# A selective-scan layer on one core: channels in four groups of 32 partitions, row and column tiles of the array, the C product on GpSimd, B left in PSUM

## The chip, the core and the metric

The kernel runs on one core of a Trainium2 chip. The metric is the device time of one execution in microseconds (us), lower being better. Five engines matter: PE (TensorE: matmuls, with its weight loads listed apart as PEld), DVE (VectorE), ACT (ScalarE), POOL (GpSimd) and SP (SyncE, which issues most of the DMAs). Each works through its own instructions in order, and they wait for one another by semaphores. PE writes its results to PSUM; the other tiles of the kernel lie in SBUF.

## What is computed

The reference is a small network on 4 images of 64 x 64 positions and 96 channels: two state-space layers ("SS2D"), then two layers of attention without softmax and a quantised feed-forward. Only the two state-space layers are touched by the change. One of them is, for every image:

```python
xz = einsum('bhwc,ec->bhwe', groupnorm(x), in_proj_w)       # 96 -> 2 x 192 channels
xx, z = split(xz, 2);  z = silu(z)
xc = silu(depthwise_conv3x3(xx) + conv_b)                   # 192 channels
for k in range(4):                # rows, columns, both backwards: u = xc in that order
    dts, Bm, Cm = split(x_proj_weight[k] @ u, [6, 22])      # 6 + 16 + 16
    delta = softplus(dt_projs_weight[k] @ dts + dt_bias[k]) # 192 channels
    h = exp(delta * A) * h + delta * Bm * u                 # 192 channels x 16 states, step by step
    y += sum_over_states(h * Cm) + Ds[k] * u
x = x + out_proj(layernorm(y) * z)
```

All of it is in float32. The recurrence for h runs over the 4096 positions of an image, in 4 directions, for 192 channels with 16 states each.

## The kernel before

**Staging.** `ssm_layer` runs twice, each time over 4 images. Per image there is `conv` (groupnorm, then the input projection and the depthwise convolution as one 3x3 convolution of nine matmuls per output, giving `xc`), then 32 steps (4 directions k x 8 chunks c of TC = 512 positions), then `finish` (layernorm, gate, output projection, residual). The attention and feed-forward layers follow in `token_layers`.

**Layout.** The 192 inner channels are two halves h of C = 96, on 96 partitions. A scan tile has 128 partitions: EG = 8 channels x 16 states, for 512 positions. A half has NJ = 12 scan tiles, so a chunk has 24, and the kernel has 2 x 4 x 32 x 24 = 6144.

**`chunk_inputs`** prepares one chunk. Four matmuls give B and C, each row repeated for the 8 channels of a scan tile (L216); ACT copies both to the SBUF tile `bc` (L220). Four more give the raw step (L225), and softplus is made of it by ACT (L239 to L243), DVE (L244) and two POOL instructions (L245, L247): `delta`. DVE multiplies `delta` by u (L250), and one DMA writes that to DRAM (`scratch`, L252). The views of u have steps of one element in directions 0 and 2, and of a whole row in directions 1 and 3.

**`scan_chunk`** does the 24 scan tiles. Every four tiles one DMA brings `dur`, delta * u spread over the states (L264). Per tile j:

- L272, PE: `da` = `rep[:, j]` x `delta`: a matmul of 96 rows that copies the 8 channels of tile j to their 128 partitions;
- L273, ACT: `da` = exp(`da` x A), in place in PSUM;
- L275, DVE: `st` = `dur` x B;
- L277, DVE: the scan itself, `st` = `da` h + `st`; L281, ACT, keeps the last column as `carry` for the next chunk;
- L282, DVE: `st` = `st` x C;
- L283, PE: `y_ps` += `sel` x `st`: sums the 16 states and puts the 8 channels in their places among the 96 (twelve matmuls accumulate).

At the end of a half DVE adds `y_ps` to `y` (L297; L293 in direction 0).

**Order.** The source calls `chunk_inputs` of the next chunk before `scan_chunk` of this one. The order on each engine is fixed when the program is built, by the framework's scheduler, which lists instructions by the order of the source and by when their operands and buffers would be ready. Waits and buffer counts decide the rest: `da` has 3 PSUM buffers, `y_ps` 2, the pair of B and C (and the pair of raw steps) one buffer of two PSUM banks, the pool `p_one` 1; `st` has 4 SBUF buffers, `dur` 3, `delta` and `bc` 2. That is all 8 PSUM banks.

**In the trace** every float32 matmul appears as two passes with a weight load each, so 6144 matmuls are listed as x12288.

Of the kernel before, what the change touches and what calls it, by code (L numbers as in the profile page):

```python
# [18 lines left out]
B = 4            # images  # L19
HW = 64          # rows and columns of an image  # L20
L = HW * HW      # positions of an image
C = 96           # model channels
E = 192          # inner channels of the scan, as two halves of C
NS = 16          # states per inner channel
R = 6            # rank of the step projection
K = 4            # scan directions
PAD = HW + 2
TC = 512         # positions per chunk
NC = L // TC
ROWS = TC // HW  # L30
EG = 8           # inner channels of one scan tile: 8 channels x 16 states
NJ = C // EG     # scan tiles per half
JG = 4           # scan tiles whose inputs one load brings
HID = 384        # FFN
# [6 lines left out]
def scan_view(t, k, c):  # L41
    """Chunk c of the scan order of direction k, of a tile [C, 2, L] in image order:
    [C, 2, ROWS, HW]. 0: rows; 1: columns; 2, 3: the same backwards."""
    part, half = t.ap[0], t.ap[1]
    if k == 0:
        off, steps = TC * c, (HW, 1)
    elif k == 1:
        off, steps = ROWS * c, (1, HW)
    elif k == 2:
        off, steps = L - 1 - TC * c, (-HW, -1)  # L50
    else:
        off, steps = L - 1 - ROWS * c, (-1, -HW)
    return bass.AP(t.tensor, t.offset + off, [part, half, [steps[0], ROWS], [steps[1], HW]])


def rows(t):
    """The last dim, of TC positions, as ROWS x HW."""
    if len(t.shape) == 2:
        return t.rearrange("p (r w) -> p r w", w=HW)
    return t.rearrange("p h (r w) -> p h r w", w=HW)  # L60


class Consts:
    def __init__(self, nc, pool, a):
# [4 lines left out]

        self.rep = load("rep", [C, NJ, 128])  # L70
        self.sel = load("sel", [128, C + NJ - 1])
        self.group = load("group", [C, C])
        self.mask = load("mask", [C, C])
        self.mean_e = pool.tile([C, C], F32, name="mean_e")
        nc.vector.memset(self.mean_e, 1.0 / E)
# [8 lines left out]
def neg_rsqrt(nc, cst, var, ln, r, sq):  # L84
    """r = -(var + EPS) ** -0.5: an exponential's first guess and one Newton step."""
    nc.scalar.activation(ln, var, AF.Ln, bias=cst.eps[:C])
# [7 lines left out]
def ssm_layer(ctx: ExitStack, tc, cst, a, pre, x_in, x_out):  # L94
    """x_out = x_in + SS2D(groupnorm(x_in)), images as [C, L]."""
# [8 lines left out]
    p_y = ctx.enter_context(tc.tile_pool(name=pre + "p_y", bufs=2, space=PSUM))  # L104
    p_two = ctx.enter_context(tc.tile_pool(name=pre + "p_two", bufs=1, space=PSUM))
    p_one = ctx.enter_context(tc.tile_pool(name=pre + "p_one", bufs=1, space=PSUM))

# [1 line left out]
    in_w = wp.tile([C, 2 * E], F32, name="in_w")  # L109
    nc.sync.dma_start(in_w, a[pre + "in_proj_w"])  # L110
    taps = wp.tile([C, 9, E], F32, name="taps")
    nc.sync.dma_start(taps, a[pre + "conv_w"].unsqueeze(0).broadcast_to([C, 9, E]))
    conv_b = wp.tile([C, 2], F32, name="conv_b")
    nc.sync.dma_start(conv_b, a[pre + "conv_b"])
    dt_b = wp.tile([C, K, 2], F32, name="dt_b")
    nc.sync.dma_start(dt_b, a[pre + "dt_projs_bias"])
    ds_k = wp.tile([C, 2, K], F32, name="ds_k")
    nc.sync.dma_start(ds_k, a[pre + "Ds"])
    gam = wp.tile([C, 2], F32, name="gam")
    nc.sync.dma_start(gam, a[pre + "gamma"])  # L120
    bet = wp.tile([C, 2], F32, name="bet")
    nc.sync.dma_start(bet, a[pre + "beta"])
    out_w = wp.tile([C, 2, C], F32, name="out_w")
    nc.sync.dma_start(out_w, a[pre + "out_proj_w"])
    a_col = wp.tile([128, K, 2, NJ], F32, name="a_col")
    nc.sync.dma_start(a_col, a[pre + "A_logs"])
    xp_t = wp.tile([C, K, 2, R + 2 * NS], F32, name="xp_t")
    nc.sync.dma_start(xp_t, a[pre + "x_proj_t"])
    xp_dt = wp.tile([R, K, E], F32, name="xp_dt")
    nc.sync.dma_start(xp_dt, a[pre + "x_proj_dt"])  # L130
    dt_w = wp.tile([R, K, E], F32, name="dt_w")
    nc.sync.dma_start(dt_w, a[pre + "dt_projs_weight"])

    # The input projection and the depthwise convolution are one 3x3 convolution.
    nc.vector.tensor_tensor(
        taps, taps, in_w[:, :E].unsqueeze(1).broadcast_to([C, 9, E]), ALU.mult
    )
    # A = -exp(A_logs), a column for each scan tile.
    nc.scalar.activation(a_col, a_col, AF.Exp)
    nc.vector.tensor_scalar_mul(a_col, a_col, -1.0)  # L140
    ds = wp.tile([C, 2], F32, name="ds")
    nc.vector.tensor_reduce(ds, ds_k, AX.X, ALU.add)
    # B and C come out of the projection once for each of a scan tile's channels.
    bc_w = wp.tile([C, K, 2, 2, 128], F32, name="bc_w")
    dl_w = wp.tile([C, K, 2, E], F32, name="dl_w")
    for k in range(K):
        for h in range(2):
            nc.vector.tensor_copy(
                bc_w[:, k, h].rearrange("p m (n e) -> p (m n) e", e=EG),
                xp_t[:, k, h, R:].unsqueeze(2).broadcast_to([C, 2 * NS, EG]),  # L150
# [3 lines left out]
                ps[:C, :E], xp_dt[:, k, h * C : (h + 1) * C], dt_w[:, k, :], start=True, stop=True  # L154
            )
            nc.scalar.copy(dl_w[:, k, h], ps[:C, :E])
# [3 lines left out]
    def conv(b):  # L160
        """Groupnorm, projection, convolution and silu: xc, [C, 2, L]."""
# [12 lines left out]
        # Means over a group's channels: of the means, then of the squares around that.  # L174
# [16 lines left out]
        xc = big.tile([C, 2, L], F32, name="xc")  # L191
        for c in range(NC):
            for h in range(2):
                ps = p_one.tile([128, TC], F32, name="ps1")
                for tap in range(9):
                    dy, dx = divmod(tap, 3)
                    nc.tensor.matmul(  # L197
                        rows(ps[:C]),
                        taps[:, tap, h * C : (h + 1) * C],
# [5 lines left out]
                    xc[:, h, c * TC : (c + 1) * TC], ps[:C], AF.Silu, bias=conv_b[:, h : h + 1]  # L205
# [3 lines left out]
    def chunk_inputs(xc, k, c):  # L209
        """Of one chunk of a direction, in scan order: the steps delta, B and C, and in  # L210
        DRAM delta * u."""
        u = scan_view(xc, k, c)
        bc_ps = p_two.tile([128, 2, TC], F32, name="ps2")
        for m in range(2):
            for h in range(2):
                nc.tensor.matmul(  # L216
                    rows(bc_ps[:, m]), bc_w[:, k, h, m], u[:, h], start=h == 0, stop=h == 1
                )
        bc = cp.tile([128, 2, TC], F32, name="bc", bufs=2)
        nc.scalar.copy(bc, bc_ps)  # L220

        raw = p_two.tile([128, 2, TC], F32, name="ps2")
        for m in range(2):
            for h in range(2):
                nc.tensor.matmul(  # L225
                    rows(raw[:C, m]),
                    dl_w[:, k, h, m * C : (m + 1) * C],
                    u[:, h],
                    start=h == 0,
                    stop=h == 1,  # L230
                )
        # softplus(s) = max(s, 0) + log1p(e), e = exp(-|s|); with w = 1 + e as it rounds,
        # log1p(e) = ln(w) + (e - (w - 1)).
        top = cp.tile([C, 2, TC], F32, name="t0")
        e = cp.tile([C, 2, TC], F32, name="t1")
        ln = cp.tile([C, 2, TC], F32, name="t2")
        w = cp.tile([C, 2, TC], F32, name="t3")
        for m in range(2):
            nc.scalar.activation(top[:, m], raw[:C, m], AF.Relu, bias=dt_b[:, k, m : m + 1])  # L239
            nc.scalar.activation(e[:, m], raw[:C, m], AF.Abs, bias=dt_b[:, k, m : m + 1])  # L240
        nc.scalar.activation(e, e, AF.Exp, scale=-1.0)
        nc.scalar.activation(ln, e, AF.Ln, bias=cst.one[:C])  # L242
        nc.scalar.activation(w, e, AF.Identity, bias=cst.one[:C])  # L243
        nc.vector.scalar_tensor_tensor(w, w, -1.0, e, ALU.add, ALU.subtract)  # L244
        nc.gpsimd.tensor_tensor(ln, ln, w, ALU.subtract)  # L245
        delta = cp.tile([C, 2, TC], F32, name="delta", bufs=2)
        nc.gpsimd.tensor_tensor(delta, top, ln, ALU.add)  # L247
        du = cp.tile([C, 2, TC], F32, name="du")
        for h in range(2):
            nc.vector.tensor_tensor(rows(du[:, h]), rows(delta[:, h]), u[:, h], ALU.mult)  # L250
        scratch = dp.tile([2, C, TC], F32, name="scratch")
        nc.sync.dma_start(scratch.rearrange("h q t -> q h t"), du)  # L252
        return bc, delta, scratch

    def scan_chunk(k, c, bc, delta, scratch, carry, xc, y):
        """h = exp(delta A) h + delta u B along the chunk, partitions being 16 states x 8
        channels; y += C h, summed over the states on the tensor engine."""
        src = scratch.rearrange("h (e j) t -> h e j t", j=NJ)
        for h in range(2):
            y_ps = p_y.tile([128, TC], F32, name="y_ps")  # L260
            for j in range(NJ):
                if j % JG == 0:
                    dur = cp.tile([128, JG, TC], F32, name="dur", bufs=3)
                    nc.sync.dma_start(  # L264
                        dur.rearrange("p j t -> p (j t)"),
                        src[h, :, j : j + JG, :]
                        .rearrange("e j t -> e (j t)")
                        .unsqueeze(0)
                        .broadcast_to([NS, EG, JG * TC]),
                    )  # L270
                da = p_da.tile([128, TC], F32, name="da")
                nc.tensor.matmul(da, cst.rep[:, j], delta[:, h], start=True, stop=True)  # L272
# [300 lines left out]
```

## Time and profile before

| | |
|---|---|
| time, median of 3 runs | 21090.39 us (21075.26 to 21090.78) |
| span of the profiled execution, first to last instruction | 21085.4 us |
| busy: PE, DVE, ACT, POOL | 18224.8, 17258.1, 8714.3, 1244.7 us |
| mean granted clock of TensorE | 0.914 |
| DMA, mean over the span | 85 GB/s |

No time of the profiled execution apart from its span is listed; the span lies 5 us under the median of the runs. The profile's pages give the busy time of each engine, groups of instructions by line with their mean duration, the idle time ahead of them and what ended it, and a chain of waits: followed back from the last instruction, at each step to what released it. A matmul's end is modelled, not measured, so a busy PE need not be PE at its peak: the distance from one pass's start to the next one's is the safer reading.

### The profile page before, as it was taken

The page shows a single profiled execution, that of the slowest core. Times are in us where ns is not written, and L with a number is a line of the kernel's source. Part 1 is how long each engine was busy: PE and PEld are TensorE (multiplying, and loading weights), DVE is VectorE, ACT ScalarE, POOL GpSimd, SP SyncE. Part 2 cuts the span into 40 slices and gives each one's busy share as a digit, 9 for nine tenths or more (in the row PEclk, how much of TensorE's full clock was granted, in tenths as well). Part 3 has the DMA queues.
Part 4 walks back from the last instruction along what each step waited for, and adds up shares of the span by engine and source line. Part 5 has one row for each costly group of instructions (what it writes and reads, how often), then busy time and mean ns, then how long its engine had stood idle before and what let it go on. Part 6 is the DMA issues. An engine that isn't in the chain of part 4 may idle for free.

```text
span 21085.4 us, 115668 instructions
## 1 busy us (share of the span) xinstructions
PE 18224.8 (86%) x34144; PEld 5598.9 (27%) x34144; DVE 17258.1 (82%) x21566; ACT 8714.3 (41%) x15985; POOL 1244.7 (6%) x556
## 2 busy tenths in 40 slices
PE   8989889998989889897899889898898988998554
PEld 2222222222222222222222222222222222222222
DVE  6999599995999679995999869995899959997333
ACT  3444344443444344443444434443444434444555
POOL 0000000000000000000000000000000000000000
PEclk9999899998999899998999999998999989998666
DMA  3444244442444234442444334442444424443000
GB/s 85 99 102 98 57 102 100 101 94 62 100 101 100 64 92 98 102 97 60 100 100 100 87 71 100 101 98 59 100 99 102 98 54 101 100 101 74 14 6 6
DMA packets 352144, 1785.52 MB, mean 85 GB/s; under 512 B 85022, under 2 KB 86240, under 8 KB 154136
## 3 DMA queue, kind: packets, MB, share of 16 engines
q1 hardware_dynamic: 344344, 1765.54, 36.6%
q10 hardware_dynamic: 7168, 12.59, 0.2%
q8 instruction: 271, 4.44, 0.1%
q14 instruction: 361, 2.96, 0.1%
HBM read 1658.45 MB, written 119.54 MB: 84 GB/s over the span
## 4 chain that ended last, share of the span: by engine, by line
DVE 57%; PE 19%; ACT 14%; issue 9%; POOL 1%; DMA 0%; SPq 0%; ACTq 0%; DVEq 0%; POOLq 0%
DVE st L277 26%; DVE st L282 13%; DVE st L275 13%; PE ps L225 5%; PE ps L197 5%; PE da L272 2%; PE y_ps L283 2%; DVE du L250 1%; ACT L242 1%; ACT L273 1%; ACT t L239 1%; ACT L87 1%; ACT t L242 1%; ACT t L243 1%; ACT t L240 1%
## 5 line engine op out<-in xcount | busy, mean ns | idle before, releaser
L272 PE MATMUL da<-delta,rep 96*128 96x512 f32 x12288 | 6845.6, 646 | 779.6 <-DVE st L277 535.4
L283 PE MATMUL y_ps<-st,sel 128*96 128x512 f32 x12288 | 6623.4, 641 | 792.1 <-DVE st L282 661.9
L277 DVE TENSOR_TENSOR_SCAN st<-da,carry,st 128x512 f32<-128x512 f32 x5376 | 6745.7, 1270 | 143.8 <-ACT da L273 142.9
L273 ACT ACTIVATE da<-da,a_col 128x512 f32<-128x512 f32 x6144 | 4012.0, 660 | 4513.1 <-PE da L272 4500.9
L275 DVE TENSOR_TENSOR st<-dur,bc 128x512 f32<-128x512 f32 x6144 | 4035.2, 672 | 527.6 <-PE y_ps L283 445.4
L282 DVE TENSOR_TENSOR st<-st,bc 128x512 f32<-128x512 f32 x6144 | 4419.2, 733 | 30.1 <-ACT carry L281 27.6
L272 PEld LDWEIGHTS da<-delta,rep 96*128 96x128 f32 x12288 | 2058.4, 194 | 5583.1 <-DVE st L277 4298.6
L283 PEld LDWEIGHTS y_ps<-st,sel 128*96 128x96 f32 x12288 | 1815.2, 170 | 5393.4 <-DVE st L282 4274.6
L281 ACT COPY carry<-st 128x1 f32<-128x1 f32 x5376 | 1021.8, 191 | 4961.8 <-DVE st L277 4954.2
L245 POOL TENSOR_TENSOR t<-t,t 96x1024 f32<-96x1024 f32 x256 | 613.1, 2395 | 17479.5 <-DVE t L244 17418.4
L216 PE MATMUL ps<-xc,bc_w 96*128 96x512 f32 x2048 | 1417.2, 812 | 0.0
L225 PE MATMUL ps<-xc,dl_w 96*96 96x512 f32 x2048 | 1368.2, 813 | 0.0
L244 DVE SCALAR_TENSOR_TENSOR t<-t,t 96x1024 f32<-96x1024 f32 x256 | 312.5, 1221 | 1156.2 <-ACT t L243 1155.3
L197 PE MATMUL ps<-xn,taps 96*96 96x512 f32 x2304 | 1040.2, 606 | 31.0 <-DVE xn L190 24.8
L277 DVE TENSOR_TENSOR_SCAN st<-da,st 128x512 f32<-128x512 f32 x768 | 903.1, 1205 | 18.6 <-ACT da L273 18.6
L247 POOL TENSOR_TENSOR delta<-t,t 96x1024 f32<-96x1024 f32 x256 | 599.3, 2341 | 20.1
L216 PEld LDWEIGHTS ps<-xc,bc_w 96*128 96x128 f32 x2048 | 398.9, 195 | 690.3 <-issue 688.1
L225 PEld LDWEIGHTS ps<-xc,dl_w 96*96 96x96 f32 x2048 | 351.4, 173 | 860.5 <-issue 779.3
L197 PEld LDWEIGHTS ps<-xn,taps 96*96 96x96 f32 x2304 | 370.6, 165 | 683.4 <-issue 565.6
L250 DVE TENSOR_TENSOR du<-delta,xc 96x512 f32<-96x512 f32 x512 | 417.1, 853 | 158.0 <-POOL delta L247 158.0
L239 ACT ACTIVATE t<-ps,dt_b 96x512 f32<-96x512 f32 x512 | 347.5, 679 | 389.6 <-PE ps L225 389.1
L89 DVE SCALAR_TENSOR_TENSOR t<-ps,t 96x512 f32<-96x512 f32 x64 | 44.0, 687 | 534.2 <-ACT t L88 534.2
(117 smaller groups left out, 7565.8 us busy)
## 6 DMA issues: line engine op xcount, KB each, us to landing
dur<-scratch SPq DMA_DIRECT2D x1536, 1024.0 KB, 7.1
scratch<-du SPq DMA_DIRECT2D x256, 384.0 KB, 3.0
xr<-in_x SPq DMA_DIRECT2D x64, 192.0 KB, 2.5
x<-xr ACTq DMA_DIRECT2D x64, 192.0 KB, 2.1
xr<-x SPq DMA_DIRECT2D x64, 192.0 KB, 2.5
xn<-in_x SPq DMA_DIRECT2D x32, 192.0 KB, 3.9
xn<-x SPq DMA_DIRECT2D x32, 192.0 KB, 5.1
t<-x SPq DMA_DIRECT2D x4, 1536.0 KB, 8.9
```

The lines of the kernel that those rows point to most:

```text
L197: nc.tensor.matmul(rows(ps[:C]), taps[:, tap, h * C : (h + 1) * C], xn[:, ROWS * c + dy : ROWS * (c + 1) + dy, dx : dx + HW], start=tap == ...
L216: nc.tensor.matmul(rows(bc_ps[:, m]), bc_w[:, k, h, m], u[:, h], start=h == 0, stop=h == 1)
L225: nc.tensor.matmul(rows(raw[:C, m]), dl_w[:, k, h, m * C : (m + 1) * C], u[:, h], start=h == 0, stop=h == 1,)
L245: nc.gpsimd.tensor_tensor(ln, ln, w, ALU.subtract)
L250: nc.vector.tensor_tensor(rows(du[:, h]), rows(delta[:, h]), u[:, h], ALU.mult)
L272: nc.tensor.matmul(da, cst.rep[:, j], delta[:, h], start=True, stop=True)
L273: nc.scalar.activation(da, da, AF.Exp, scale=a_col[:, k, h, j : j + 1])
L275: nc.vector.tensor_tensor(st, dur[:, j % JG], bc[:, 0], ALU.mult)
L277: nc.vector.tensor_tensor_scan(st, da, st, 0.0 if c == 0 else col, ALU.mult, ALU.add)
L281: nc.scalar.copy(col, st[:, TC - 1 : TC])
L282: nc.vector.tensor_tensor(st, st, bc[:, 1], ALU.mult)
L283: nc.tensor.matmul(y_ps[:C], cst.sel[:, NJ - 1 - j : NJ - 1 - j + C], st, start=j == 0, stop=j == NJ - 1,)
```

## The change

The 192 channels are laid out anew: two halves of P = 128 partitions, each of NT = 4 groups of 32 partitions of which 24 carry channels (NB = 3 blocks of 8) and 8 are zero padding. Weights are padded on the host accordingly. Tile j = i * NT + t is block i of group t. Then:

- the matmul that makes `da` reads only the 32 partitions of group t (32 rows x 128 columns: a row tile of the array at row 32 t);
- the matmul that sums the states writes only the 32 partitions of group t (128 rows x 32 columns: a column tile), and three of them accumulate where twelve did;
- the product with C goes from DVE (L282) to POOL;
- B is not copied to SBUF: DVE reads it in PSUM, where it stays for the whole chunk in one of two buffers; C alone is copied (512 elements instead of 1024);
- `scratch` is written by four DMAs of 24 partitions instead of one of 96; `dur` comes in loads of the same size as before;
- PSUM: `y_ps` has 1 buffer instead of 2, `p_one` 2 instead of 1 (it now serves C, the raw steps, the convolution, the gate and the layernorm), the two-bank pool goes, B has 2.
- everything on the 96 partitions of a half of the inner channels is now on 128, over the same number of elements per partition.

```diff
-EG = 8           # inner channels of one scan tile: 8 channels x 16 states
-NJ = C // EG     # scan tiles per half
-JG = 4           # scan tiles whose inputs one load brings
+EG = 8
+NT = 4
+NB = 3
+NJ = NT * NB
+P = 128
...
-        self.rep = load("rep", [C, NJ, 128])
-        self.sel = load("sel", [128, C + NJ - 1])
+        self.rep = load("rep", [P, NB, 128])
+        self.sel = load("sel", [128, NB, 32])
...
-    p_y = ctx.enter_context(tc.tile_pool(name=pre + "p_y", bufs=2, space=PSUM))
-    p_two = ctx.enter_context(tc.tile_pool(name=pre + "p_two", bufs=1, space=PSUM))
-    p_one = ctx.enter_context(tc.tile_pool(name=pre + "p_one", bufs=1, space=PSUM))
+    p_y = ctx.enter_context(tc.tile_pool(name=pre + "p_y", bufs=1, space=PSUM))
+    p_b = ctx.enter_context(tc.tile_pool(name=pre + "p_b", bufs=2, space=PSUM))
+    p_one = ctx.enter_context(tc.tile_pool(name=pre + "p_one", bufs=2, space=PSUM))
...
-        bc_ps = p_two.tile([128, 2, TC], F32, name="ps2")
-        for m in range(2):
-            for h in range(2):
-                nc.tensor.matmul(
-                    rows(bc_ps[:, m]), bc_w[:, k, h, m], u[:, h], start=h == 0, stop=h == 1
-                )
-        bc = cp.tile([128, 2, TC], F32, name="bc", bufs=2)
-        nc.scalar.copy(bc, bc_ps)
+        b_ps = p_b.tile([128, TC], F32, name="b_ps")
+        c_ps = p_one.tile([128, TC], F32, name="ps1")
+        for m, ps in enumerate((b_ps, c_ps)):
+            for h in range(2):
+                nc.tensor.matmul(rows(ps), bc_w[:, k, h, m], u[:, h], start=h == 0, stop=h == 1)
+        cc = cp.tile([128, TC], F32, name="cc", bufs=2)
+        nc.scalar.copy(cc, c_ps)
...
-        scratch = dp.tile([2, C, TC], F32, name="scratch")
-        nc.sync.dma_start(scratch.rearrange("h q t -> q h t"), du)
+        scratch = dp.tile([2, NB * EG, NT, TC], F32, name="scratch")
+        for t in range(NT):
+            nc.sync.dma_start(
+                scratch[:, :, t].rearrange("h q l -> q h l"), du[32 * t : 32 * t + NB * EG]
+            )
...
-            y_ps = p_y.tile([128, TC], F32, name="y_ps")
-            for j in range(NJ):
...
-                nc.tensor.matmul(da, cst.rep[:, j], delta[:, h], start=True, stop=True)
-                nc.scalar.activation(da, da, AF.Exp, scale=a_col[:, k, h, j : j + 1])
-                st = sp.tile([128, TC], F32, name="st")
-                nc.vector.tensor_tensor(st, dur[:, j % JG], bc[:, 0], ALU.mult)
...
-                nc.vector.tensor_tensor(st, st, bc[:, 1], ALU.mult)
-                nc.tensor.matmul(
-                    y_ps[:C],
-                    cst.sel[:, NJ - 1 - j : NJ - 1 - j + C],
-                    st,
-                    start=j == 0,
-                    stop=j == NJ - 1,
-                )
+            y_ps = p_y.tile([P, TC], F32, name="y_ps")
+            for i in range(NB):
...
+                for t in range(NT):
+                    j = i * NT + t
+                    part = slice(32 * t, 32 * t + 32)
+                    da = p_da.tile([128, TC], F32, name="da")
+                    nc.tensor.matmul(
+                        da, cst.rep[part, i], delta[part, h], start=True, stop=True
+                    )
+                    nc.scalar.activation(da, da, AF.Exp, scale=a_col[:, k, h, j : j + 1])
+                    st = sp.tile([128, TC], F32, name="st")
+                    nc.vector.tensor_tensor(st, dur[:, t], b_ps, ALU.mult)
...
+                    nc.gpsimd.tensor_tensor(st, st, cc, ALU.mult)
+                    nc.tensor.matmul(
+                        y_ps[part], cst.sel[:, i], st, start=i == 0, stop=i == NB - 1
+                    )
```

## The prediction

> **What bounds the kernel now.** I read the page from the top: the engines' shares, the chain of waits by engine, the groups by line (their last two columns: mean ns of one, and idle time ahead of it with what ended it).
>
> ```profile
> PE 18224.8 (86%) x34144; PEld 5598.9 (27%) x34144; DVE 17258.1 (82%) x21566; ACT 8714.3 (41%) x15985; POOL 1244.7 (6%) x556
> ...
> DVE 57%; PE 19%; ACT 14%; issue 9%; POOL 1%; DMA 0%; SPq 0%; ACTq 0%; DVEq 0%; POOLq 0%
> ...
> L272 PE MATMUL da<-delta,rep 96*128 96x512 f32 x12288 | 6845.6, 646 | 779.6 <-DVE st L277 535.4
> L283 PE MATMUL y_ps<-st,sel 128*96 128x512 f32 x12288 | 6623.4, 641 | 792.1 <-DVE st L282 661.9
> L277 DVE TENSOR_TENSOR_SCAN st<-da,carry,st 128x512 f32<-128x512 f32 x5376 | 6745.7, 1270 | 143.8 <-ACT da L273 142.9
> ...
> L275 DVE TENSOR_TENSOR st<-dur,bc 128x512 f32<-128x512 f32 x6144 | 4035.2, 672 | 527.6 <-PE y_ps L283 445.4
> L282 DVE TENSOR_TENSOR st<-st,bc 128x512 f32<-128x512 f32 x6144 | 4419.2, 733 | 30.1 <-ACT carry L281 27.6
> ...
> L245 POOL TENSOR_TENSOR t<-t,t 96x1024 f32<-96x1024 f32 x256 | 613.1, 2395 | 17479.5 <-DVE t L244 17418.4
> ```
>
> PE is busy longest, but the chain names DVE, and PE's loads wait for DVE (L272 for the scan, L283 for L282). POOL is idle. To know whether the whole span is like that I cut it by stage. The first image's chunks 2 to 32 are this line of the windows table (columns: window, its length, busy time of PE, PEld, DVE, ACT, POOL, clock, DMA share, GB/s):
>
> ```profile
> 236.30:2313.70 2077.40, 1890.73 (x3462) 557.51 (x3460) 1959.97 (x2394) 874.09 (x1701) 142.66 (x60) 0.96 0.43 99
> ```
>
> A chunk takes 2077.4 / 31 = 67.0 us, DVE being busy 63.2 of it and idle 3.8. The other images give the same, so 8 x 32 = 256 chunks are 17.15 of the 21.09 ms; convolution, finish and the token layers are the rest. The timeline then shows one scan tile:
>
> ```profile
> 2022.23 1.12 PE L272 MATMUL da<-delta,rep 96*128 96x512 f32 x2
> 2022.68 0.68 DVE L282 TENSOR_TENSOR st<-st,bc 128x512 f32<-128x512 f32 x1
> 2023.29 1.27 DVE L277 TENSOR_TENSOR_SCAN st<-da,carry,st 128x512 f32<-128x512 f32 x1
> ...
> 2023.42 1.10 PE L283 MATMUL y_ps<-st,sel 128*96 128x512 f32 x2
> 2024.48 0.66 DVE L275 TENSOR_TENSOR st<-dur,bc 128x512 f32<-128x512 f32 x1
> ...
> 2024.61 1.12 PE L272 MATMUL da<-delta,rep 96*128 96x512 f32 x2
> ```
>
> Two starts of L272 are 2.38 us apart: scan 1.19, L275 0.58 and L282 0.60 from start to start, without a gap on DVE. The two matmuls fill 2.22 of the 2.38, each standing alone, started by DVE. So DVE sets the pace and PE is a close second: what is taken off DVE is worth only as much as PE can follow.
>
> **What the change takes off DVE.** L282 goes: 24 x 0.60 = 14.4 us a chunk. With it goes a stall that the mean of 733 ns hides:
>
> ```profile
> 2062.55 2.34 POOL L247 TENSOR_TENSOR delta<-t,t 96x1024 f32<-96x1024 f32 x1
> ...
> 2063.11 2.34 DVE L282 TENSOR_TENSOR st<-st,bc 128x512 f32<-128x512 f32 x1
> ```
>
> The 240 runs of L282 that overlap a POOL instruction took 2.09 us in the mean, the other 5904 took 0.68; 480 scans inside POOL's work took 1.264 against 1.262 us. L282 reads two tiles in SBUF, the scan one in SBUF and `da` in PSUM. B in PSUM gives L275 the scan's kind of operands, so I cost the collision of the 24 new POOL products with scan and L275 at nothing. If that cover fails, 24 tiles could each wait up to a POOL product.
>
> What is left per chunk on DVE: 24 x (1.19 + 0.60) = 43.0. L275 from PSUM is not in the trace; the nearest rows, products with one PSUM operand (L405, L460: 686, 684 ns on 96x512), say +12 ns, from below 0: 24 x 0.012 = 0.3. Then L244 1.2, L250 2 x 0.85, L297 0.65 or 1.23 twice: 5.0 together. The first two still read two SBUF tiles and can meet a POOL product, at most 1.2 us each, 3 x 0.6 = 1.8. Sum 50.1; with today's 3.8 idle (largely ACT's softplus block, unchanged) 53.9 us.
>
> **POOL.** The product of 128x512 is not in the trace. Half of L247 (2341 ns for 1024 elements) is 1.17 us, all of it 2.34 if the time were fixed. I take 1.2, as time by elements is what every other engine's rows show (ACT 660 against 1016 ns on 512 and 1024): 24 x 1.2 + 4.7 = 33.5 us a chunk, hidden beside DVE. L245 and L247 queue behind it for at most a few products; they belong to the next chunk. A scan's result now passes POOL before L283, some 0.6 us later than today; four `st` buffers cover it.
>
> **PE.** This is what ends last. Dense passes start 0.429 us apart, so four cost 1.716 a tile. Inputs add 16 passes a chunk: 0.429 each in directions 0 and 2 (6.9), 0.858 in 1 and 3, where u has steps of a row (13.7): mean 10.3. Today PE has one shape of array; after it `da` is 32 rows x 128 columns, `y_ps` 128 x 32, so the shape changes between nearly every two matmuls. No row shows that price. Below: nothing (dense, 1.716 a tile). Above: every matmul alone, as in the timeline: L272 0.533 to its second pass and 0.592 for that one, 1.125; L283 with a 32-column load 0.026 + 0.429 + 0.592 = 1.047 (the exposed load is 0.104 for 128 columns, 0.078 for 96): 2.17 a tile, 0.23 a change. A whole pass, 0.429, is the farthest row that I use. In the trace 24% of matmuls follow one of their own kind; if the order stays like that, 1.52 changes a tile remain: 1.716 + 1.52 x 0.23 = 2.07. Neighbours of one kind use different row or column groups and might overlap by up to a pass, 2 x 0.24 x 0.43 = 0.2 less: 1.86. I take 2.0, nearer to the row of matmuls alone, since alternation rules the order in the timeline. PE per chunk: 48.0 + 6.9 or 13.7, plus 3.8 idle = 58.7 or 65.5, mean 62.1, against DVE's 53.9.
>
> The Trainium skill, "TensorEngine Tiling (Array Packing)", Key Properties, speaks against this change: changing the mode, not just the tile, drains the array. No row here shows a mode change; by that rule the sum would lie at the 2.07 to 2.17 end. The skill's "TensorE: Matmul & The Clock Gate", Part 3, speaks for it: four row tiles measured 3.07 times faster. That needs four of one kind in a row, which three `da` buffers and the alternation do not give.
>
> **The rest.** `p_one` with two buffers takes the convolution's wait for its eviction (PE loads of L197 on ACT: 97.9 us in all): -0.1 ms. `finish` goes through the same tiles one after the other: 0. Four scratch DMAs cost SP three issues of 0.31 more; SP is idle and `dur` is late for only 81 us in all: 0. One `y_ps` buffer makes the next half's first sum wait for L297, twice a chunk; four `st` let DVE run on 7 us meanwhile: 0, at worst 2 x 1.2 a chunk. ACT copies 512 elements less, 0.35 off 28 us: 0.
>
> **Sum.** 256 x (62.1 - 67.0) = -1254 us, -100: span 21085 - 1354 = 19731, and the 5 us by which the runs' median exceeds the span: **19740 us**. With 1.86 to 2.17 a tile: 18.9 to 20.8 ms.
>
> **Rivals.**
> 1. *The change of shape is free, DVE sets the pace.* Even directions 53.9, odd 54.9 (PE, 41.2 + 13.7) + 3.8 = 58.7, mean 56.3: 18.25 ms; with neighbours overlapping 53.9 throughout, 17.6. For it: passes of different weights stream without a gap today. Against: nothing today shows two shapes together.
> 2. *Slower: the change of shape costs a whole pass.* It lies between L272 and L283, 1.52 times a tile: 1.716 + 1.52 x 0.429 = 2.37, 24 x 2.37 + 10.3 + 3.8 = 71.0 a chunk: +1.0 ms, 22.0 ms. It decides from 0.33 us a change, where PE reaches today's 67 us; that is only 0.1 above my price.
> 3. *POOL bounds* with 2.34 us a product: 24 x 2.34 + 4.7 + 3.8 = 64.7: 20.4 ms. Against: elements set the time elsewhere.
> 4. *It doesn't do what it says*: row and column tiles never run side by side because kinds alternate. That is inside my forecast, which gives overlap only 0.07 a tile.
>
> **How the numbers follow.** My case 0.42, free switch 0.25, whole pass 0.26, POOL 0.05, within 0.2% 0.02 (about what a measurement of this kernel tells from no change). Faster 0.42 + 0.25 + 0.05 = 0.72. The range must reach both sides' cases: 17.6 to 22.0 ms; the forecast's own is 18.9 to 20.8.
>
> **What would show it.** L282 on POOL at about 1.2 us; L275 near 0.68 with no long runs; scan unchanged at 1.27. PE's starts in a tile some 2.0 us apart, DVE with 8 to 10 us idle a chunk, ended by PE or ACT; chunks of 59 and 65 us. I am wrong if DVE stays without gaps (rival 1), if the second kind's first pass starts over 0.33 us late (rival 2), or if the granted clock in the scans leaves 0.96: at half of it all passes double.

## The result and the profile after

The changed kernel takes 22201.4 us (median of 4 runs, 22081.33 to 22376.29) against 21087.31 before: 1.0537 times as long, 95% interval 1.049 to 1.0584. The forecast was 19740 us, its range 17600 to 22000.

The page of the changed kernel, with the lines that answer to those shown of before (PEclk is the granted clock of TensorE in 40 slices, in tenths; the product with C is now L283 on POOL):

```profile
PE 19429.3 (88%) x34144; PEld 4519.9 (20%) x34144; DVE 13624.4 (62%) x15421; ACT 8606.1 (39%) x16193; POOL 9052.5 (41%) x6700
...
PEclk9878888888887788887887788787886878887666
...
PE 46%; issue 23%; POOL 20%; ACT 7%; DVE 4%; DMA 0%; POOLq 0%; SPq 0%; DVEq 0%; ACTq 0%
...
L283 POOL TENSOR_TENSOR st<-st,cc 128x512 f32<-128x512 f32 x6144 | 7833.7, 1291 | 9047.4 <-ACT carry L282 7365.4
L284 PE MATMUL y_ps<-st,sel 128*32 128x512 f32 x12288 | 7110.2, 753 | 924.6 <-POOL st L283 881.5
L278 DVE TENSOR_TENSOR_SCAN st<-da,carry,st 128x512 f32<-128x512 f32 x5376 | 6735.9, 1275 | 1788.4 <-ACT da L274 1785.8
L271 PE MATMUL da<-delta,rep 32*128 32x512 f32 x12288 | 7128.3, 776 | 329.8 <-DVE st L278 265.8
...
L276 DVE TENSOR_TENSOR st<-dur,b_ps 128x512 f32<-128x512 f32 x6144 | 3983.6, 675 | 1618.8 <-PE y_ps L284 1611.2
```

DVE is relieved as planned: 82% of the span has become 62%, the scan and the product with B are as long as before. The chain has gone over to PE. But the same 12288 passes of L271 and L284 have grown, from 646 and 641 ns to 776 and 753, and the clock row points to the reason: 9 in nearly every slice of the scans before, mostly 7 and 8 now. The windows table, for chunks 2 to 32 of the first image (window, its length, busy PE, PEld, DVE, ACT, POOL, clock, DMA share, GB/s):

```profile
263.90:2423.80 2159.90, 2013.28 (x3466) 414.01 (x3464) 1513.05 (x1643) 863.39 (x1728) 1084.56 (x802) 0.83 0.42 95
```

A chunk is 2159.9 / 31 = 69.7 us here and 70.65 over all images, against 66.98; the clock is 0.83 (0.813 over all images), against 0.96. It switches between full and half. The timeline of PE at full clock, with the shape changing at every matmul:

```profile
2001.49 1.05 PE L284 MATMUL y_ps<-st,sel 128*32 128x512 f32 x2
2002.47 1.12 PE L271 MATMUL da<-delta,rep 32*128 32x512 f32 x2
2003.52 1.04 PE L284 MATMUL y_ps<-st,sel 128*32 128x512 f32 x2
```

and in a stretch at half clock:

```profile
1185.36 1.92 PE L284 MATMUL y_ps<-st,sel 128*32 128x512 f32 x2
1187.20 2.07 PE L271 MATMUL da<-delta,rep 32*128 32x512 f32 x2
1189.20 1.92 PE L284 MATMUL y_ps<-st,sel 128*32 128x512 f32 x2
```

From one L284 to the next, a tile costs PE 2.03 us at full clock, what the forecast took (2.0), and 3.84 at half. So the price of the shapes was about right and the clock was not. Two theories: **(1)** the small shapes themselves lower the clock; **(2)** PE's waits do, behind POOL, the one `y_ps` and the four `st` buffers, whatever the shapes.

### The profile page after: what moved, and what is told of

Read it like the earlier page. It is cut to its first block, busy times and chain, and to the rows that moved or that the text cites. A ratio compares the mean times of both kernels' runs of the same rounds, so it can differ in the third digit from the quotient of the medians.

```text
span 22079.6 us, 127759 instructions
## 1 busy us (share of the span) xinstructions
PE 19429.3 (88%) x34144; PEld 4519.9 (20%) x34144; DVE 13624.4 (62%) x15421; ACT 8606.1 (39%) x16193; POOL 9052.5 (41%) x6700
## 4 chain that ended last, share of the span: by engine, by line
PE 46%; issue 23%; POOL 20%; ACT 7%; DVE 4%; DMA 0%; POOLq 0%; SPq 0%; DVEq 0%; ACTq 0%
POOL st L283 17%; PE y_ps L284 15%; PE da L271 15%; PE ps L194 5%; PE ps L227 4%; PE b_ps L214 2%; POOL delta L242 1%; POOL t L240 1%; ACT da L274 1%; ACT L88 1%; PE y_ps L338 1%; DVE st L278 1%; PE ps L325 1%; PE ps L214 1%; PE pa L400 1%
## 5 line engine op out<-in xcount | busy, mean ns | idle before, releaser
L283 POOL TENSOR_TENSOR st<-st,cc 128x512 f32<-128x512 f32 x6144 | 7833.7, 1291 | 9047.4 <-ACT carry L282 7365.4
L284 PE MATMUL y_ps<-st,sel 128*32 128x512 f32 x12288 | 7110.2, 753 | 924.6 <-POOL st L283 881.5
L271 PE MATMUL da<-delta,rep 32*128 32x512 f32 x12288 | 7128.3, 776 | 329.8 <-DVE st L278 265.8
L274 ACT ACTIVATE da<-da,A_logs 128x512 f32<-128x512 f32 x6144 | 4019.9, 661 | 8247.7 <-PE da L271 8229.8
L276 DVE TENSOR_TENSOR st<-dur,b_ps 128x512 f32<-128x512 f32 x6144 | 3983.6, 675 | 1618.8 <-PE y_ps L284 1611.2
L271 PEld LDWEIGHTS da<-delta,rep 32*128 32x128 f32 x12288 | 1855.8, 218 | 6275.8 <-issue 3163.8
L284 PEld LDWEIGHTS y_ps<-st,sel 128*32 128x32 f32 x12288 | 851.7, 118 | 6404.3 <-POOL st L283 4229.6
L227 PE MATMUL ps<-xc,dl_w 128*128 128x512 f32 x2048 | 1622.8, 899 | 73.7 <-ACT t L235 73.7
L282 ACT COPY carry<-st 128x1 f32<-128x1 f32 x5376 | 933.4, 187 | 1312.3 <-DVE st L278 1301.7
L194 PE MATMUL ps<-xn,taps 96*128 96x512 f32 x2304 | 999.5, 596 | 5.4 <-DVE xn L187 5.4
L214 PE MATMUL ps<-xc,bc_w 128*128 128x512 f32 x1024 | 834.9, 915 | 0.0
```

The costliest lines, as they stand in the source:

```text
L194: nc.tensor.matmul(rows(ps), taps[:, tap, h * P : (h + 1) * P], xn[:, ROWS * c + dy : ROWS * (c + 1) + dy, dx : dx + HW], start=tap == 0, ...
L214: nc.tensor.matmul(rows(ps), bc_w[:, k, h, m], u[:, h], start=h == 0, stop=h == 1)
L227: nc.tensor.matmul(rows(raw), dl_w[:, k, h, m * P : (m + 1) * P], u[:, h], start=h == 0, stop=h == 1,)
L271: nc.tensor.matmul(da, cst.rep[part, i], delta[part, h], start=True, stop=True)
L274: nc.scalar.activation(da, da, AF.Exp, scale=a_col[:, k, h, j : j + 1])
L276: nc.vector.tensor_tensor(st, dur[:, t], b_ps, ALU.mult)
```

## The experiments

All but the two benches compute everything. Order matters: in the traces `after` (the changed kernel), `col_tile_only` and `row_tile_64` have the same instructions in the same order on PE, DVE, ACT and POOL, entry by entry, as far as the traces name them; so have `full_shapes` and `row_tile_only` (another order), and `row_pairs` and `col_pairs` (a third). Within each of the three sets only the shape of the `da` matmul differs. Ratios are to before, with 95% intervals; chunk and clock are means over the scans of all images.

| kernel | time, us | ratio | chunk, us | clock |
|---|---|---|---|---|
| before | 21087 | 1 | 66.98 | 0.958 |
| after: rows 32, columns 32 | 22201 | 1.0537 (1.049 to 1.0584) | 70.65 | 0.813 |
| row_tile_64: rows 64, columns 32 | 20485 | 0.9717 (0.9703 to 0.9732) | 64.06 | 0.955 |
| col_tile_only: rows 128, columns 32 | 19915 | 0.9447 (0.9433 to 0.9461) | 61.94 | 0.993 |
| full_shapes: whole array for both | 21704 | 1.0294 (1.0277 to 1.0311) | 68.72 | 0.979 |
| row_tile_only: rows 32, columns 128 | 24428 | 1.159 (1.1573 to 1.1607) | 79.40 | 0.755 |
| b_in_sbuf | 21067 | 0.9991 (0.9982 to 1.0) | 66.42 | 0.992 |
| c_on_dve | 21040 | 0.998 (0.9971 to 0.999) | 65.88 | 0.992 |
| col_da4_st8 | 20974 | 0.9947 (0.9933 to 0.9962) | 64.73 | 0.967 |
| row_pairs: rows 32 | 27539 | 1.3065 (1.3043 to 1.3087) | 91.06 | 0.634 |
| col_pairs: rows 128 | 22497 | 1.0671 (1.0655 to 1.0687) | 71.58 | 0.942 |
| col_st6 | 19884 | 0.9432 (0.9418 to 0.9446) | 61.86 | 0.993 |

**full_shapes, row_tile_only, col_tile_only: undo the small shapes, both or one.** From the changed kernel, `full_shapes` has both of these edits, `col_tile_only` the first, `row_tile_only` the second (with constants of the same zeros and ones spread over the whole array):

```diff
-                        da, cst.rep[part, i], delta[part, h], start=True, stop=True
+                        da, cst.rep[:, j], delta[:, h], start=True, stop=True
...
-                        y_ps[part], cst.sel[:, i], st, start=i == 0, stop=i == NB - 1
+                        y_ps, cst.sel[:, j], st, start=j == 0, stop=j == NJ - 1
```

> Theory 1 (the shapes lower the clock): matmuls of 32 rows or 32 columns count as little activity of the array, so the clock is halved although PE has work. With both matmuls on the whole array, the clock in the scans comes back to 0.94 or more, a tile costs PE 1.72 us, and the kernel takes 18.3 to 19.3 ms. Theory 2 (the waits lower the clock): PE stands idle behind POOL's product, the single y_ps buffer and the four st buffers, and the idle stretches halve the clock whatever the shapes. Then the clock stays under 0.88 and the time falls by no more than the cheaper passes, to 20.0 to 21.8 ms.

> Row tiles for da, whole array for the sum. Theory 1: half of the passes count as full activity, so clock and time lie between those of the changed kernel and of full_shapes: clock 0.86 to 0.92, 19.5 to 21 ms. Theory 2: as many changes of shape and the same waits as in the changed kernel: clock 0.78 to 0.84, 21.7 to 22.6 ms.

> Whole array for da, column tiles for the sum. Theory 1: as for the row tiles alone, clock 0.86 to 0.92, 19.5 to 21 ms; the two together show which shape it is. Theory 2: clock 0.78 to 0.84, 21.7 to 22.6 ms.

Neither theory had it whole: `full_shapes` has the clock of theory 1 and the time of theory 2, and the clocks of the other two lie outside both theories' ranges, one below and one above. The windows of chunks 2 to 32, of `col_tile_only`, `row_tile_only` and `full_shapes`:

```profile
257.10:2176.20 1919.10, 1780.62 (x3467) 429.01 (x3465) 1511.62 (x1642) 871.44 (x1728) 1079.44 (x802) 0.99 0.47 107
```

```profile
268.50:2729.40 2460.90, 2171.28 (x3448) 625.35 (x3442) 1593.85 (x1636) 847.92 (x1696) 1106.94 (x802) 0.75 0.36 83
```

```profile
256.30:2390.30 2134.00, 1814.66 (x3446) 612.68 (x3444) 1571.16 (x1637) 857.23 (x1696) 1108.38 (x802) 0.98 0.41 96
```

The clock goes with the rows, in both orders: 0.99 and 0.98 where `da` uses 128 rows, 0.83 and 0.75 where it uses 32. Column tiles do no harm to it. At equal order the row tiles cost 22201 - 19915 = 2286 us and 24428 - 21704 = 2724 us. Theory 1 falls for the columns and stands for the rows. Theory 2 keeps a part: `full_shapes` has its clock back and is still slower than before. Its waits (us in total, times, longest; PEld is the weight load, PE the matmul itself):

```profile
PEld y_ps L284 <- POOL st L283: 7666.9, 6058, 3.3
...
PE y_ps L284 <- POOL st L283: 2340.9, 2952, 2.5
```

Ahead of the sum PE's loads wait 7.7 ms for POOL's product there, and PE itself stands idle for 2.3 ms; in `col_tile_only` it is 3.8 and 0.79 ms (4.2 and 0.88 in the changed kernel). On PE nothing passes a sum that waits, so the next `da` waits too. In `full_shapes` the scheduler set the instructions in another order; how much of the 1.8 ms between it and `col_tile_only` is the order and how much the shape was not separated.

**array_bench: the shapes by themselves.**

> Leaves out the whole network: eight stretches of matmuls alone, the output being a copy of x. 1: shapes of before, dense, alternating; 2: shapes of after, alternating; 3: one row tile; 4: one column tile; 5: four row tiles in turn; 6: four column tiles in turn; 7 and 8: a matmul, a copy on ACT, a matmul, in whole and in small shapes. Theory 1: clock 1.0 in stretch 1, near 0.5 in 2, 3 and 4; in 8 lower than in 7. Theory 2: 1.0 in 1 to 6, and 7 and 8 alike. Either way: two matmuls take 1.72 us in stretch 1 and 2.02 in 2 at full clock, and four row tiles in turn take about 0.25 us each if they run side by side, 0.96 if not.

Its windows, stretch by stretch (columns as above, without DVE):

```profile
5.30:282.60 277.30, 277.30 (x640) 112.91 (x640) 0.00 (x0) 0.00 (x0) 1.00 0.15 45
282.60:606.90 324.30, 324.30 (x641) 68.75 (x640) 0.00 (x0) 0.00 (x0) 1.00 0.00 0
606.90:1150.30 543.40, 543.40 (x642) 211.22 (x641) 0.00 (x0) 0.00 (x0) 0.50 0.00 0
1150.30:1426.30 276.00, 276.00 (x645) 70.50 (x644) 0.00 (x0) 0.00 (x0) 1.00 0.00 0
1426.30:1563.80 137.50, 137.50 (x1281) 65.48 (x1280) 0.00 (x0) 0.00 (x0) 1.00 0.00 1
1563.80:1701.30 137.50, 137.50 (x1285) 41.50 (x1281) 0.00 (x0) 0.00 (x0) 1.00 0.01 1
1701.30:2131.40 430.10, 313.32 (x644) 99.81 (x640) 93.78 (x160) 0.00 (x0) 1.00 0.00 0
2131.40:2872.20 740.80, 623.99 (x641) 108.16 (x640) 93.76 (x160) 0.00 (x0) 0.50 0.00 0
```

Stretches 1 and 2: 320 matmuls each, 0.867 and 1.013 us apiece, so a change of shape costs 0.15 us and a tile 2.03; the clock stays at 1.0. Stretch 3: one row tile, without a gap, at half clock throughout, PE being busy all the time. Stretch 4: one column tile, full clock. 5 and 6: four tiles in turn, 640 matmuls in 137.5 us, 0.215 apiece: four truly run side by side, at full clock. 7 and 8: the same waits, other shapes: 1.0 and 0.5. Waits alone don't decide, and busy PE alone doesn't either.

**clock_bench: rows against busy time.**

> Leaves out the whole network: sixteen stretches of some 150 us, the output being a copy of x. A unit is 1, 2, 4 or 8 matmuls of 128 columns behind a copy on ACT that the next unit waits for, each with 128, 96, 64 and 32 rows, all in the first row tile. If the clock follows rows x busy time over a window: with 128 rows it stays 1.0 from 2 matmuls a unit on; with 64 rows it is near the edge, falling with fewer matmuls a unit; with 32 rows it is 0.5 throughout, even with 8 a unit. If it follows busy time alone: the same clock for the same number of matmuls a unit, whatever the rows.

Windows with 128 rows (1 and 8 matmuls a unit; 2 and 4 are at 1.00 as well), with 96 rows (1, 2, 4 and 8) and with 64 rows (1 and 8; 2 and 4 are at 0.50 as well). The four with 32 rows, which come last, are all at 0.50:

```profile
5.60:151.40 145.80, 92.14 (x161) 24.70 (x161) 47.24 (x79) 0.00 (x0) 1.00 0.27 83
...
437.30:570.30 133.00, 121.11 (x274) 50.40 (x273) 10.15 (x17) 0.00 (x0) 1.00 0.00 0
570.30:781.70 211.40, 157.14 (x162) 37.95 (x160) 47.77 (x80) 0.00 (x0) 0.53 0.00 0
781.70:1021.70 240.00, 200.56 (x213) 62.37 (x214) 31.64 (x53) 0.00 (x0) 0.50 0.00 0
1021.70:1164.60 142.90, 119.80 (x257) 46.64 (x256) 19.11 (x32) 0.00 (x0) 0.99 0.00 0
1164.60:1297.60 133.00, 121.10 (x273) 50.17 (x271) 10.15 (x17) 0.00 (x0) 1.00 0.00 0
1297.60:1514.60 217.00, 162.65 (x161) 39.27 (x160) 47.84 (x80) 0.00 (x0) 0.51 0.00 0
...
2007.70:2258.00 250.30, 238.12 (x273) 87.56 (x271) 10.16 (x17) 0.00 (x0) 0.50 0.00 0
```

With one matmul behind each wait 128 rows keep the full clock, and 96 rows win it back with four. With 64 rows it is lost at once and not won back, even with eight and PE busy 95% of the time; whether eight would keep a full clock that they start with was not run. The expectation for 64 rows ("near the edge") missed in that they were below it at once. So what holds the clock goes with rows times busy time, and the kernels agree roughly. A chunk has 112 passes of 0.427 us at full clock, 47.8 us; with the 48 passes of `da` weighted by rows / 128 the share of the chunk is 46% in the changed kernel (32.4 / 70.65), 59% in `row_tile_64`, 77% in `col_tile_only`, with clocks 0.813, 0.955, 0.993. Unweighted, `after` and `col_pairs` are alike (68% and 67%) while their clocks are 0.813 and 0.942. But a mean over a chunk is too coarse to order them all: `col_pairs` has a larger weighted share than `row_tile_64`, 67%, and a lower clock.

The traces show the rule in finer steps. In all 14 of them the granted clock changes only at multiples of 3.41 us. Take each such window of the scans and the benches, and as its share rows / 128 times the time in which passes stream (half as much for time at half clock), divided by 3.41 us. Of the windows at full clock, all 1955 with a share under 0.32 were followed by half clock, and all but 53 of the 45567 with 0.40 or more by full clock. One cut at 0.375 errs in 461 of all 49157; the best cut by busy time alone errs in 1576. At half clock a window holds only half as much, and of the 6544 there with a share under 0.30 none was followed by full clock. So a clock once lost is hard to win back: one tile of the changed kernel, two passes of 32 rows and two of 128, comes to 0.53 in its 2.03 us at full clock, but to 0.28 in its 3.84 us at half. This stretch of the changed kernel stays at half clock although PE is busy all the time:

```profile
1186.00:1226.00 40.00, 40.00 (x48) 7.45 (x46) 21.53 (x23) 13.46 (x26) 12.73 (x11) 0.50 0.28 63
```

**row_tile_64: half the way.** As `col_tile_only`, but with the 64 rows of two groups:

```diff
+                    two = slice(64 * (t // 2), 64 * (t // 2) + 64)
...
+                        da, cst.rep[two, j], delta[two, h], start=True, stop=True
```

> The changed kernel, but da is made on tiles of 64 rows x 128 columns (two groups, the other group's weights being zero). Theory 1, now for row tiles alone: the fewer rows of the array a pass uses, the less it counts as activity, so 64 rows give a clock between 0.81 (32 rows) and 0.99 (128 rows, col_tile_only): 0.88 to 0.96 in the scans and 20.2 to 21.3 ms. Rival: row tiles run side by side, PE is done sooner and its idle stretches lower the clock, whatever the number of rows: clock 0.80 to 0.85 and 21.8 to 22.5 ms.

20485 us, between the two, at the same order: 32, 64 and 128 rows give 22201, 20485 and 19915 us. Its rival (idle time after overlap) is out.

**b_in_sbuf and c_on_dve: the two other parts, one at a time**, from `col_tile_only`:

```diff
+        bb = cp.tile([128, TC], F32, name="bb", bufs=2)
+        nc.scalar.copy(bb, b_ps)
...
-        return b_ps, cc, delta, scratch
+        return bb, cc, delta, scratch
```

```diff
-                    nc.gpsimd.tensor_tensor(st, st, cc, ALU.mult)
+                    nc.vector.tensor_tensor(st, st, cc, ALU.mult)
```

> col_tile_only, with B copied to SBUF as before. If products with two SBUF inputs on DVE collide with POOL's work as L282 did in the trace of before, L276 goes from 0.68 to a mean of 1.0 us or more and the time from 19.9 to 20.8 to 22.5 ms. If the forecast's cost of nothing holds without B in PSUM too, 19.8 to 20.0 ms.

> col_tile_only, with the product with C back on DVE (no POOL products). If the work taken off DVE is what gained, DVE is the bound again with 63 us busy a chunk: 20.7 to 21.2 ms. If the way through POOL costs as much as it saves, 19.7 to 20.2 ms.

Both first alternatives held. The groups of `b_in_sbuf`:

```profile
L285 POOL TENSOR_TENSOR st<-st,cc 128x512 f32<-128x512 f32 x6144 | 9037.4, 1486 | 6549.1 <-ACT carry L284 5313.6
...
L278 DVE TENSOR_TENSOR st<-dur,bb 128x512 f32<-128x512 f32 x6144 | 7368.6, 1231 | 302.3 <-PE y_ps L286 298.6
```

With both operands in SBUF the product with B takes 1231 ns instead of 672, and POOL's 1486 instead of 1288: 1.15 ms, about all that the move to POOL gained. Before the change, with POOL mostly idle, the product with B took 672 ns with both operands in SBUF too (L275), so it is POOL's work beside it that counts. With C back on DVE, DVE is busy 62.2 us a chunk again and the gain is gone as well: 1.12 ms. (Both edits also moved some instructions.)

**row_pairs and col_pairs: meant to put row tiles side by side.** Two neighbouring `da` in one tile of two PSUM banks, one behind the other in the source (`p_da` 2 such buffers, `p_one` 1):

```diff
+                    if t % 2 == 0:
+                        da2 = p_da.tile([128, 2, TC], F32, name="da")
+                        for s in range(2):
+                            two = slice(32 * (t + s), 32 * (t + s) + 32)
+                            nc.tensor.matmul(
+                                da2[:, s], cst.rep[two, i], delta[two, h], start=True, stop=True
+                            )
+                    da = da2[:, t % 2]
```

`col_pairs` has `cst.rep[:, j + s], delta[:, h]` there.

> The changed kernel, with the da of two neighbouring groups made by two row-tile matmuls one behind the other into a tile of two PSUM banks (two such tiles, p_one 1 buffer). If row tiles side by side count together as activity, as four in turn did in the array bench (clock 1.0), the clock in the scans rises from 0.81 to about that of row_tile_64, 0.93 to 0.97, and each pair costs PE one matmul less: chunk 55 to 62 us, 18.5 to 20.3 ms. If a row tile lowers the clock however it is issued: clock below 0.86 and above 21.5 ms.

> As row_pairs, in the same order of instructions on every engine, but da is made with the whole array, so the two matmuls of a pair follow one another. If overlap is what row tiles are worth, this is slower than row_pairs by up to 12 x 0.86 us = 10 us a chunk, 2.6 ms; if PE's time for da does not end last, the two agree within 0.3 ms, or row_pairs loses by its clock.

`row_pairs` is the slowest of all: the first alternative is a clear miss, the second held. But the pairs did not stay together. In its trace 15% of the `da` matmuls follow another one, against 18% in the changed kernel; between the others the scheduler put a sum or an input, as here:

```profile
2010.78 1.12 PE L274 MATMUL da<-delta,rep 32*128 32x512 f32 x2
2011.83 1.99 PE L227 MATMUL ps<-xc,dl_w 128*128 128x512 f32 x4
2013.74 1.04 PE L288 MATMUL y_ps<-st,sel 128*32 128x512 f32 x2
2014.72 1.12 PE L274 MATMUL da<-delta,rep 32*128 32x512 f32 x2
```

So whether two row tiles that do run side by side hold the clock was not tested. What the two kernels show is the effect of the rows once more, in a third order. Windows of chunks 2 to 32, `row_pairs` and `col_pairs`:

```profile
305.40:3128.30 2822.90, 2612.99 (x3477) 491.78 (x3476) 1555.26 (x1643) 870.06 (x1738) 1101.26 (x804) 0.63 0.32 73
```

```profile
280.20:2500.00 2219.80, 1912.68 (x3477) 437.80 (x3475) 1541.12 (x1644) 883.95 (x1738) 1096.49 (x804) 0.94 0.41 93
```

The sum of rows times time over the chunk is what it was, 32.4 us, while the chunk of this order is longer by itself (71.6 in `col_pairs` against 61.9). By the rule above that is a smaller share, so a lower clock, so a longer chunk again; this chain is argued, no run separates its links. Four row tiles in turn, which did run side by side, kept the clock in the bench, with nothing else between them.

**col_da4_st8 and col_st6: more buffers for the best version.** `col_tile_only` with `p_da` 4, `p_one` 1 and `sp` 8, and with `sp` 6 alone:

```diff
-    sp = ctx.enter_context(tc.tile_pool(name=pre + "scan", bufs=4))
+    sp = ctx.enter_context(tc.tile_pool(name=pre + "scan", bufs=6))
```

> col_tile_only with 4 buffers of da (p_one 1) and 8 of st. If the round scan, POOL, sum, next da, exponential through three da buffers holds the chunk at 61.9 us, the chunk falls to PE's own 57 to 59 us: 18.7 to 19.4 ms. If PE's passes themselves bound it, 19.7 to 20.0 ms.

> col_tile_only with 6 buffers of st instead of 4, all else alike (only some instructions change places). If the st buffers hold the round through POOL, the chunk falls from 61.9 towards 58: 18.9 to 19.6 ms. If not, 19.7 to 20.1 ms.

Neither helps as hoped. `col_da4_st8` is outside both of its ranges and 5% slower than `col_tile_only`: its chunk is 64.7 us, and the rest of the kernel, with one `p_one`, 0.3 ms longer; several things differ, its order too, and this was not taken apart. `col_st6` takes 19884 us, within the range of "not". PE is busy 57.4 of 61.9 us a chunk in `col_tile_only`, and the chain of waits there names PE for 41%, POOL for 24%: it is mostly PE that ends last. `col_st6` and `col_tile_only` are the fastest versions; `row_tile_64` beats both kernels too.

## Why the prediction was wrong, step by step

- **What leaves DVE: right.** 14.4 us a chunk were to go; busy time fell from 63.2 to 48.8.
- **B in PSUM at nothing: right, and shown.** L276 takes 675 ns (672 before); without PSUM it takes 1231.
- **POOL's product, 1.2 us: 1.29.** The size was right, though the ACT rows given for it (660 and 1016 ns) do not double with the elements. The way through POOL is nearly covered in this order: PE's loads for the sum wait 4.2 ms for it, as they waited 4.3 for DVE's product before, and PE itself stands idle there for 0.88 ms against 0.66. In the order of `full_shapes` it is 2.3 ms.
- **The price of a change of shape, 0.23 us and 2.0 us a tile: the sum right, its parts not.** Measured 0.15 and 2.03; same-kind neighbours do overlap at times.
- **The sum at PE's pace.** With that order, that price and a clock of 0.993, `col_tile_only` gives 61.94 us a chunk where the forecast said 62.1, and 19915 us where it said 19740. That is so close partly by luck: the forecast's 3.8 us of idle time were DVE's of before, while PE's idle time here is 4.5 us, 3.1 of it behind POOL's product.
- **The step that failed: "PE. This is what ends last. Dense passes start 0.429 us apart".** PE does end last, but the 0.429 carried today's clock over to passes of 32 rows. In the changed kernel the clock is 0.813 in the scans, and a tile costs 3.84 us in its half-clock stretches. At equal order the row tiles cost 2286 us, 19915 to 22201, with what they gain by overlap already taken off: nearly all of the 2461 us by which the forecast missed. The forecast named a falling clock only among the things that would make it wrong, without a price or a chance. The trace of before had a warning: 0.61 in the window of `finish`, where PE's matmuls are few.
- **Rival 2** gave 22.0 ms, close to what came, by another mechanism; a change of shape costs 0.15 us, not 0.43, so the agreement is an accident. (By the forecast's own terms its break-even is 0.32 us a change, not 0.33.)
- **The rest, -0.1 ms: about 0.05 longer in the profiled execution.** The convolution fell from 143.3 to 124.9 us an image, but the first chunk after it grew from 66.2 to 102.2, as its inputs no longer run among the convolution's matmuls.

The Trainium skill ("TensorE: Matmul & The Clock Gate", Part 1) describes the gate as watching how busy PE has been and passing half or all of the clock. The runs agree on the two values, and add the rows: a dense stream of 32 rows stayed at 0.50. Its Part 3 gives 3.07 for four row tiles; here four in turn took 0.215 us a matmul (stretch 5) against 0.867 on the whole array (stretch 1), 4.0 times less, both at full clock.

## What to carry to other kernels

Before a matmul is cut to fewer rows, work out rows / 128 times the share of time that PE streams, for the stage, and look at its thin stretches too: where PE has waits, a few rows can cost the full clock for every other matmul of the stage as well. Where a row tile saves little by overlap, padding it to 128 rows with zero weights costs no time by itself (a tile took 2.03 us at full clock with 32 rows and with 128) and keeps the clock. Moving an elementwise product to GpSimd paid here only while DVE's other product read one operand from PSUM; with both in SBUF the gain was gone.

## What the runs showed of the hardware that was not expected

- A single row tile of 32 rows lost the full clock with PE busy 100% of the time; one of 64 rows did not win it back with PE busy 95%. 96 rows won it back with 4 matmuls behind each wait, not with 2; 128 rows kept it with 1. A dense column tile of 32 columns kept it as well (1.00).
- The clock changes only at multiples of 3.41 us, and a window at full clock keeps it from some 0.375 of rows times streaming time on. At half clock a window holds half as much, so a mix of shapes can stay at half clock with PE always busy.
- Four row tiles or four column tiles in turn run wholly side by side: 0.215 us a matmul. In the changed kernel three `da` did so as well at times, six passes in 1.24 us, where one matmul takes 1.12:

```profile
925.54 1.24 PE L271 MATMUL da<-delta,rep 32*128 32x512 f32 x6
```

- A change of shape between row and column tiles costs some 0.15 us in a dense stream, no more.
